# A written order of TensorE, VectorE and ScalarE in both attentions of a two-layer transformer kernel

## Chip, cores and metric

The kernel runs on one core of one Trainium2 chip. The metric is the device time in microseconds (us) of one execution. PE is TensorE, DVE VectorE, ACT ScalarE, POOL GpSimd, SP SyncE.

## What is computed

Eight sequences of 512 tokens with 256 features pass through two layers. Each layer is attention and then routed experts, each behind a layer norm and added to its input:

```python
x = x + _L0_attn_ref(_layernorm(x), Wq, Wk, Wv, Wo)      # 16 heads of 16, 4 kv heads, rope, causal
x = x + _L0_ffn_ref(_layernorm(x), router_w, ...)        # 32 experts, 8 for a token
x = x + _L1_attn_ref(_layernorm(x), w_qkv, b_qkv, ...)   # 16 heads of 16, causal
x = x + _L1_ffn_ref(_layernorm(x), gate_w, ...)          # 16 experts, 2 for a token, and a shared one
```

The softmax of the attention is computed as the exponential of the scores, a causal mask by multiplication, a product with v that has a column of ones beside it, and a division by that column's result.

## The kernel before, in words

**Stages.** A preamble of some 31 us, attention 0 with the router of layer 0, the experts of layer 0, attention 1 with the router and the shared expert of layer 1, the experts of layer 1 with the output. The change touches the two attentions. The experts run with their TensorE instructions in written order (L1173); everything else is put in order by a scheduler at compile time, which takes the program's order as a starting point and fills each engine's queue as it thinks fit. [...]

**Attention.** Both layers use the class `Attention` (L615 to L731). A sequence is done in four groups c of four heads (NCK = 4, NG = 4). The keys lie in four blocks j of 128; `BANKS = [[0], [1, 3], [2]]` puts them in three steps n[...]: j = 0 has 512 queries, 1 and 3 have 384 and 128, 2 has 256. A step is `scores` (L628): for each block four matmuls, one for each head, on 32 rows of the array each, so that four run side by side (L638), and one exponential over all four heads (L643) from PSUM tile `st`, of which there is one; then `mask` (L646): a multiplication of the diagonal blocks by the causal mask on DVE (L649). The tiles p of steps 0 and 1 share a tag with two buffers, that of step 2 has one.

`values` (L653) of a group: sixteen matmuls into `o` (L661; four for each block, on 32 columns each, so that four run side by side), a copy of `o` to SBUF on DVE (L667), four transposes to token order (L674), the reciprocal of the sums (L677), and the multiplication (L678 and on). It yields after each block, after the copy and at the end, and `steps` (L684) takes one such piece after the scores and one before the mask of each step of the next group. `output` (L707) of a sequence: two small operations on `fine` (L712, L713), transposes (L719) and copies (L720) to `oT`, the product with the output weights `y` (L727) and its addition to x (L731).

**Fills.** `pipeline` (L734) goes through the sequences. While the groups of sequence b run, it calls piece by piece `before(b + 1)` (the next sequence's load, layer norm, q, k and v) and `finish(b - 1)` (`output` and then `after`, the layer norm for the experts and the router of the sequence before). How many pieces have been made at which step is a matter of counts: `n_before` and `n_after` yields spread over the steps.
- `before` of layer 0 (L828): transposes of the input and copies `x_in` on ACT, layer norm, xT, `qkv` (L843), the rotation on DVE (L850 to L865, for each of four tiles of 128 tokens), transposes and copies of q and k (L873 to L883). Of layer 1 (L926): addition of the gathered experts' result (L932), layer norm, v (L941, L945), q (L954), k (L959 to L963).
- `layernorm` (L281): statistics of four tiles (bn_stats, bn_aggr, L286 to L288), `inverse_root` (L266; twelve small DVE operations, shift and three Newton steps), four tiles `xn` (L292). `turned` (L302): transposes to xT and copies on ACT.
- `route` (L314): logits `lg` (L321), the maximum (L327), an exponential on ACT (L336), choosing the best, the ranks `rk` by matmul (L368, L370), keys and row numbers (L382), and indirect DMAs on POOL that scatter the normalized rows `xn_f` to the experts' buffers (L385): 32 a sequence in layer 0, 8 in layer 1. The tag `xn_rows` has two buffers in layer 0 and one in layer 1.
- `shared` (L393), in layer 1: the shared expert, after `route`, with Silu on ACT (L406).
- `ahead1` in attention 1: for sequence b + 3, a fetch of its x, a part of a weight load, and `gathers` (L1197), that is row numbers on DVE and 32 indirect DMAs on POOL (L1200).

After the last sequence, its own `finish` runs with nothing beside it; the experts' loads of weights `dw` are issued after the last product with v.

Of the kernel before, what the change touches and what calls it, by code (L numbers as in the profile page):

```python
# [16 lines left out]
P = 128  # L17
# [55 lines left out]
STEPS = 2 * len(BANKS)  # L73
# [17 lines left out]
def two_blocks_kernel(  # L91
# [78 lines left out]
    def biases1(tmp, bank):  # L170
# [8 lines left out]
        yield  # L179
# [18 lines left out]
        yield  # L198
# [67 lines left out]
    def inverse_root(var, lnp, name):  # L266

        v = lnp.tile([P, NT], F32, tag="v", name=f"v_{name}")
        nc.vector.tensor_scalar(v, var, LN_EPS, None, ALU.add)
        bits = lnp.tile([P, NT], I32, tag="bits", name=f"bits_{name}")  # L270
        nc.vector.tensor_scalar(bits, v.bitcast(I32), 1, None, ALU.arith_shift_right)
        r = lnp.tile([P, NT], F32, tag="rstd", name=f"rstd_{name}")
        nc.vector.tensor_scalar(r.bitcast(I32), bits, -1.0, float(0x5F3759DF), ALU.mult, ALU.add)
        w = lnp.tile([P, NT], F32, tag="w", name=f"w_{name}")
        for _ in range(3):
            nc.vector.scalar_tensor_tensor(w, r, -0.5, r, ALU.mult, ALU.mult)
            nc.vector.tensor_tensor(w, w, v, ALU.mult)
            nc.vector.scalar_tensor_tensor(r, w, 1.5, r, ALU.add, ALU.mult)
        return r

    def layernorm(x, lnp, name, tag="xn", bufs=1, spare=0, behind=None):  # L281

# [6 lines left out]
        rstd = inverse_root(mv[:, :, 1], lnp, name)  # L289
        xn = lnp.tile([P, NT, D + spare], F32, tag=tag, name=f"xn_{name}", bufs=bufs)  # L290
        for t in range(NT):
            nc.vector.tensor_scalar(  # L292
                xn[:, t, :D], x[:, t, :], mv[:, t, 0:1], rstd[:, t : t + 1], ALU.subtract, ALU.mult
            )
        return xn

    def free():

        for _ in range(4):
            yield  # L300

    def turned(xn, lnp, bank, name):  # L302

        xT = lnp.tile([P, ND, T], F32, tag="xT", name=f"xT_{name}")
        for c in range(ND):
# [4 lines left out]
            yield  # L310
        return xT

    def ffn_parts(smp, bank):
        def route(n, b, xn, xT, name, again):  # L314
# [10 lines left out]
            yield  # L325
# [11 lines left out]
            yield  # L337
# [10 lines left out]
            yield  # L348
# [15 lines left out]
            yield  # L364
# [26 lines left out]
            yield  # L391

        def shared(w, xT, x, name):  # L393

            hs = smp.tile([P, NS, T], F32, tag="hs", name=f"hs_{name}", bufs=1)
            for n in range(NS):
# [11 lines left out]
                yield  # L408
            for half_ in range(NT // 2):
# [11 lines left out]
                yield  # L421
# [3 lines left out]
    def general_parts(awp, lnp, atp, ptp, smp, bank, vbias1=None):  # L425
# [130 lines left out]
        def attention0(b, w):  # L556
            x, name = xs[b], f"a0_{b}"
            xn = yield from turned(layernorm(x, lnp, name), lnp, bank, name)
# [34 lines left out]
        def attention1(b, w):  # L593
            x, name = xs[b], f"a1_{b}"
            xn = yield from turned(layernorm(x, lnp, name), lnp, bank, name)
# [19 lines left out]
    class Attention:  # L615
# [6 lines left out]
        def __init__(self, n, late, ptp, ps, bank, wo, masked=None):  # L622
            self.n, self.fine, self.late, self.ptp, self.ps, self.bank, self.wo = n, fines[n], late, ptp, ps, bank, wo
            self.heads, self.otok, self.rec = {}, {}, {}
            self.last = iter(())
            self.masked = masked

        def scores(self, b, c, n, probs):  # L628
# [13 lines left out]
            pt = self.ptp.tile([P, NG, width], F32, tag="p2" if n == 2 else "p01", name=f"p_{name}", bufs=1 + (n < 2))  # L642
# [10 lines left out]
        def values(self, b, c, probs):  # L653
# [4 lines left out]
            for step, j in enumerate((0, 1, 3, 2)):  # L658
# [6 lines left out]
                yield  # L665
            osb = late.tile([P, T], F32, tag="osb", name=f"osb_{name}", bufs=1)
            nc.vector.tensor_copy(osb, o)  # L667
            yield
# [4 lines left out]
            for t in range(NT):  # L673
                nc.tensor.transpose(ot[:, t * P : (t + 1) * P], osb[:, t * P : (t + 1) * P], ident)  # L674
# [7 lines left out]
            yield  # L682

        def steps(self, b):  # L684

            for c in range(NCK):  # L690
                probs = {}
                for n in range(len(BANKS)):
                    self.scores(b, c, n, probs)
                    next(self.last, None)
                    yield
                    if n == len(BANKS) - 1:
                        self.last = self.values(b, c, probs)
                    next(self.last, None)
                    yield
                    self.mask(n, probs)  # L700

        def flush(self):
            for _ in range(STEPS - 1):
                next(self.last, None)
                yield

        def output(self, b, x):  # L707
# [8 lines left out]
            for k in range(ND):  # L716
# [4 lines left out]
                yield  # L721
            for h in range(NT // 2):
# [9 lines left out]
                yield  # L732

    def pipeline(att, before, after, n_before, n_after, till, ahead=None, lead=0):  # L734
# [8 lines left out]

        n_steps = NCK * STEPS
        n_after += 4
# [939 lines left out]
```

## Time and profile before

| | |
|---|---|
| median of 3 runs | 1708.37 us (1708.31 to 1708.81) |
| the profiled execution | 1701.29 us, of which 1699.6 us span |
| PE busy | 1543.7 us, 91% of the span |
| DVE busy | 992.0 us, 58% |
| ACT busy | 650.7 us, 38% |
| POOL busy | 792.1 us, 47% |
| first scores of the eight sequences of attention 0 (us after the span's start) | 30.7, 73.5, 120.0, 164.8, 212.4, 257.8, 307.7, 351.5 |
| last product with v of attention 0 | 392.3 |
| first scores of the eight sequences of attention 1 | 884.5, 933.1, 996.1, 1059.1, 1122.2, 1191.1, 1261.9, 1324.9 |
| first transposes of layer 1's experts | 1425.5 |

The difference of two neighbours in these lists is the length of a sequence's window. An engine that is busy for nearly the whole window bounds it. A line of the timeline gives start, length, engine, source line, operation, output and inputs, shape and number of instructions, and in brackets how long the engine was idle before and what ended that.

### The profile page before, as it was taken

Reading aid. Unit: us, or ns where it says so; the run is one execution under the profiler, and the core shown is the slowest. Engines: PE = TensorE matmul, PEld = TensorE weight load, DVE = VectorE, ACT = ScalarE, POOL = GpSimd, SP = SyncE. Lnnn points to the kernel's source line nnn. Section 1 sums busy time; section 2 is a strip of 40 time slices with the busy share of each in tenths; the row PEclk is TensorE's granted clock in tenths of the full one; section 3 lists DMA queues with packets and bytes.
Section 4 is the critical chain, followed back from the end, with each engine's and each line's share of the span. In section 5 each row is a group of like instructions: output and inputs, shape, how many; then the busy total and the mean of one; then the engine's idle time right before and its main releaser. Section 6 shows DMA issues by size and latency. Waiting matters only on the chain. (4 is left out here: it accounts for less than half of the span.)

```text
span 1699.6 us, 30922 instructions
## 1 busy us (share of the span) xinstructions
PE 1543.7 (91%) x10180; PEld 1029.0 (61%) x10180; DVE 992.0 (58%) x3131; ACT 650.7 (38%) x865; POOL 792.1 (47%) x660
## 2 busy tenths in 40 slices
PE   5899999995999999999989999999899988999982
PEld 2455454543898999998853454544444545777761
DVE  5678887875555555555455764764656544444452
ACT  2555554552233333333334554454355331222221
POOL 0017677577710004888888448888511011000473
PEclk9999999997999999999999999999899998999996
DMA  2035557236988778999995245664312024343563
GB/s 73 13 87 156 163 167 270 102 139 207 307 256 269 202 201 226 266 264 273 268 194 71 39 107 80 127 136 72 86 52 79 26 84 159 109 159 116 156 225 120
DMA packets 255128, 259.43 MB, mean 153 GB/s; under 512 B 80212, under 2 KB 235988, under 8 KB 254964
## 3 DMA queue, kind: packets, MB, share of 16 engines
q1 hardware_dynamic: 199172, 167.88, 32.5%
q0 software_dynamic: 55296, 88.65, 23.0%
q8 instruction: 87, 1.43, 0.4%
q10 hardware_dynamic: 496, 0.85, 0.1%
q14 instruction: 77, 0.63, 0.1%
HBM read 132.70 MB, written 124.57 MB: 151 GB/s over the span
## 5 line engine op out<-in xcount | busy, mean ns | idle before, releaser
L1200 POOL DMA_INDIRECT x_a<-yg,yrows x256 | 402.9, 1574 | 277.2 <-DMA xg_m<-xg 181.9
L385 POOL DMA_INDIRECT xg<-xn_f,rows_f x320 | 321.2, 1004 | 414.7 <-DVE rows_f L382 197.3
L643 ACT ACTIVATE p_a<-st_a 128x2048 f32<-128x2048 f32 (+1 forms) x192 | 306.1, 1594 | 276.4 <-PE st_a L638 243.2
L1131 PE MATMUL gu_m<-gw,xgTs_m 128*128 x1552 | 335.6, 360 | 4.9 <-DVE xgTs_m L1108 3.0
L1131 PEld LDWEIGHTS gu_m<-gw,xgTs_m 128*128 128x128 f32 x1552 | 258.1, 192 | 33.9 <-DVE xgTs_m L1108 3.2
L1162 PE MATMUL y_m<-dw,hTs_m 96*128 (+1 forms) x952 | 237.7, 379 | 0.0
L638 PE MATMUL st_a<-qT_a,kT_a 32*128 32x512 f32 (+3 forms) x2048 | 202.1, 478 | 11.1 <-ACT p_a L643 10.8
L649 DVE TENSOR_TENSOR p_a<-p_a,causal 128x512 f32<-128x512 f32 x256 | 170.8, 686 | 57.3 <-ACT p_a L643 56.1
L661 PE MATMUL o_a<-p_a,v 128*32 128x512 f32 (+3 forms) x2048 | 197.4, 455 | 6.9 <-DVE p_a L649 6.7
L1108 DVE COPY xgTs_m<-xgT_m 128x512 f32<-128x512 f32 x194 | 133.9, 690 | 109.7 <-PE xgT_m L1106 109.4
L1167 ACT COPY ys_m<-y_m 128x512 f32<-128x512 f32 x194 | 113.7, 586 | 189.1 <-PE y_m L1162 174.7
L1123 DVE SCALAR_TENSOR_TENSOR h_m<-h_m,xg_m,gu_m 128x96 f32<-128x96 f32 (+1 forms) x388 | 114.8, 326 | 115.2 <-ACT h_m L1136 69.3
L1162 PEld LDWEIGHTS y_m<-dw,hTs_m 96*128 96x128 f32 (+1 forms) x952 | 165.3, 190 | 15.1
L1262 POOL DMA_INDIRECT g<-yg,yrows x64 | 65.2, 1018 | 202.2 <-DVE h_m L1123 170.9
L638 PEld LDWEIGHTS st_a<-qT_a,kT_a 32*128 32x128 f32 x2048 | 90.1, 189 | 107.2 <-issue 52.4
L1152 DVE COPY hTs_m<-hT_m 96x256 f32<-96x256 f32 (+1 forms) x194 | 92.7, 478 | 99.5 <-PE hT_m L1151 98.5
L1106 PE MATMUL xgT_m<-ident,xg_m 128*128 128x128 f32 x776 | 119.3, 275 | 16.0 <-DMA xg_m<-xg 13.2
L1139 ACT ACTIVATE h_m<-gu_m 128x192 f32<-128x192 f32 x150 | 49.7, 331 | 212.2 <-PE gu_m L1131 200.6
L1106 PEld LDWEIGHTS xgT_m<-ident,xg_m 128*128 128x128 f32 x776 | 95.6, 141 | 39.2 <-issue 16.6
L661 PEld LDWEIGHTS o_a<-p_a,v 128*32 128x32 f32 x2048 | 49.3, 110 | 107.8 <-issue 66.1
L1151 PE MATMUL hT_m<-ident,h_m 128*96 128x128 f32 (+1 forms) x476 | 84.9, 274 | 0.6 <-DVE h_m L1123 0.4
L667 DVE COPY osb_a<-o_a 128x512 f32<-128x512 f32 x64 | 44.0, 688 | 53.0 <-PE o_a L661 53.0
(198 smaller groups left out, 1689.6 us busy)
## 6 DMA issues: line engine op xcount, KB each, us to landing
yg<-ys_m SPq DMA_DIRECT2D x194, 256.0 KB
xg_m<-xg SPq DMA_DIRECT2D x300, 144.0 KB
xg_m<-xg SPq DMA_DIRECT2D x88, 136.0 KB
xg<-zeros SPq DMA_DIRECT2D x66, 144.0 KB
xg<-xn_f,rows_f POOLq DMA_INDIRECT x320
xg<-zeros SPq DMA_DIRECT2D x34, 136.0 KB
xf<-in_x_dram SPq DMA_DIRECT2D x8, 512.0 KB
x_after<-x_in SPq DMA_DIRECT2D x8, 512.0 KB
```

Of the source, the lines that this page charges most:

```text
L385: inst = nc.gpsimd.indirect_dma_start(out=lay.xg, out_offset=bass.IndirectOffsetOnAxis(ap=rows[:, t, i : i + 1], axis=0), in_=xn[:, t, :], ...
L638: nc.tensor.matmul(st[:, g, at : at + T - j * P], kT[r, j * P : (j + 1) * P], qT[r, j * P :], start=True, stop=True,)
L643: nc.scalar.activation(pt, st[:, :, :width], AF.Exp, scale=SCALE)
L649: self.masked = nc.vector.tensor_tensor(d, d, causal.unsqueeze(1).to_broadcast([P, NG, P]), ALU.mult).ins
L661: nc.tensor.matmul(o[32 * g : 32 * g + 32, j * P :], v1[:, j, v_at + g * (DH + 1) :][:, :32], probs[n][:, g, at : at + T - j * P], start=( ...
L1106: nc.tensor.transpose(tr[:, j, c, :], xg[:, j, c * P : (c + 1) * P], ident)
L1108: nc.vector.tensor_copy(xT, tr)
L1123: nc.vector.scalar_tensor_tensor(h[:, j, :], h[:, j, :], xg[:, j, D:][:, bass.ds(offs[part, i + j][2], 1)], gus[j][:, inner:], ALU.mult, A ...
L1131: nc.tensor.matmul(gus[j], xT[:, j, c, :], gu[:, bass.ds(at + c * 2 * inner, 2 * inner)], start=(c == 0), stop=(c == ND - 1),)
L1162: nc.tensor.matmul(y[:, j, :], hT[:n_in, q, j, :], dn[:n_in, bass.ds(at + q * D, D)], start=(q == 0), stop=(q == n_ch - 1),)
L1167: nc.scalar.copy(ys, y)
L1200: nc.gpsimd.indirect_dma_start(out=xs[b][:, t, :], out_offset=None, in_=yg, in_offset=rows, compute_op=ALU.add)
```

## The change

Both pipelines now stand in `tc.manual_schedule(engines={PE, DVE, Activation})`: these three engines' queues are in the order in which the program writes the instructions. POOL and SP are left to the scheduler. The program's own order changes with it:
- `values` becomes `products` (all sixteen matmuls in one go, and the copy of `o`, which moves from DVE to ACT) and `normalize` (transposes, reciprocal, multiplication). Of the group before, `products` stands after the scores of step 0 and `normalize` after those of step 1.
- A gap is the place between the scores of a step and its mask. Fills are made only in gaps 1 and 2 of a group. Each yield now carries a cost in us (negative: VectorE work on which the next piece waits; zero: nothing more in this gap). The class `Fill` counts cost against what is due at each gap, in the shares 0, 0.55 and 0.45, and at least `LEAST` is made in a gap.
- `layernorm` is a generator in six pieces: two of statistics, two of the root, two of normalizing.
- In layer 1 pieces of `route` and `shared` alternate, q and k have tiles of their own for each half (three buffers), and p of steps 0 and 1 have three buffers. `ahead` starts at gap 2 of a sequence and is called twice a gap.

The rest of the diff puts costs on yields. Its core:

```diff
@@ -70,7 +70,8 @@
 BANKS = [[0], [1, 3], [2]]
 QOFF = {0: (0, 0), 1: (1, 0), 3: (1, 3 * P), 2: (2, 0)}
-STEPS = 2 * len(BANKS)
+NGAP = NCK * len(BANKS)
+LEAST = (0.0, 1.6, 1.2)
 SUM_LO, SUM_HI = 1e-20, 1e30
@@ -286,18 +278,31 @@
             with tc.issue_after(behind) if behind else ExitStack():
                 nc.vector.bn_stats(out=stats[:, t, :], in_=x[:, t, :])
             nc.vector.bn_aggr(out=mv[:, t, :], in_=stats[:, t, :])
-        rstd = inverse_root(mv[:, :, 1], lnp, name)
+            if t % 2:
+                yield -1.1
+        v = lnp.tile([P, NT], F32, tag="v", name=f"v_{name}")
+        nc.vector.tensor_scalar(v, mv[:, :, 1], LN_EPS, None, ALU.add)
+        bits = lnp.tile([P, NT], I32, tag="bits", name=f"bits_{name}")
+        nc.vector.tensor_scalar(bits, v.bitcast(I32), 1, None, ALU.arith_shift_right)
+        r = lnp.tile([P, NT], F32, tag="rstd", name=f"rstd_{name}")
+        nc.vector.tensor_scalar(r.bitcast(I32), bits, -1.0, float(0x5F3759DF), ALU.mult, ALU.add)
+        w = lnp.tile([P, NT], F32, tag="w", name=f"w_{name}")
+        for n in range(3):
+            nc.vector.scalar_tensor_tensor(w, r, -0.5, r, ALU.mult, ALU.mult)
+            nc.vector.tensor_tensor(w, w, v, ALU.mult)
+            nc.vector.scalar_tensor_tensor(r, w, 1.5, r, ALU.add, ALU.mult)
+            if n != 1:
+                yield -1.1
         xn = lnp.tile([P, NT, D + spare], F32, tag=tag, name=f"xn_{name}", bufs=bufs)
         for t in range(NT):
             nc.vector.tensor_scalar(
-                xn[:, t, :D], x[:, t, :], mv[:, t, 0:1], rstd[:, t : t + 1], ALU.subtract, ALU.mult
+                xn[:, t, :D], x[:, t, :], mv[:, t, 0:1], r[:, t : t + 1], ALU.subtract, ALU.mult
             )
+            if t % 2:
+                yield -0.8
+        yield 0.0
         return xn
-    def free():
-        for _ in range(4):
-            yield
     def turned(xn, lnp, bank, name):
@@ -639,7 +647,7 @@
                         st[:, g, at : at + T - j * P], kT[r, j * P : (j + 1) * P], qT[r, j * P :],
                         start=True, stop=True,
                     )
-            pt = self.ptp.tile([P, NG, width], F32, tag="p2" if n == 2 else "p01", name=f"p_{name}", bufs=1 + (n < 2))
+            pt = self.ptp.tile([P, NG, width], F32, tag="p2" if n == 2 else "p01", name=f"p_{name}", bufs=3 if n < 2 else 1)
             nc.scalar.activation(pt, st[:, :, :width], AF.Exp, scale=SCALE)
             probs[n] = pt
@@ -662,16 +670,18 @@
                         o[32 * g : 32 * g + 32, j * P :], v1[:, j, v_at + g * (DH + 1) :][:, :32],
                         probs[n][:, g, at : at + T - j * P], start=(step == 0), stop=(step == NT - 1),
                     )
-                yield
-            osb = late.tile([P, T], F32, tag="osb", name=f"osb_{name}", bufs=1)
-            nc.vector.tensor_copy(osb, o)
-            yield
+            self.osb = late.tile([P, T], F32, tag="osb", name=f"osb_{name}", bufs=1)
+            nc.scalar.copy(self.osb, o)
+        def normalize(self, b, c, probs):
+            late, name = self.late, f"a{self.n}_{b}_{c}"
             if c == 0:
                 self.otok[b] = late.tile([P, NT, NCK, NG, DH], F32, tag="otok", name=f"otok_{name}", bufs=1)
                 self.rec[b] = late.tile([P, NCK, NT, NG], F32, tag="rec", name=f"rec_{name}", bufs=2)
             ot = self.bank(f"ot_{name}")
             for t in range(NT):
-                nc.tensor.transpose(ot[:, t * P : (t + 1) * P], osb[:, t * P : (t + 1) * P], ident)
+                nc.tensor.transpose(ot[:, t * P : (t + 1) * P], self.osb[:, t * P : (t + 1) * P], ident)
             ot = ot.rearrange("p (t g d) -> p t g d", t=NT, g=NG)
             rec = self.rec[b][:, c, :, :]
             nc.vector.reciprocal(rec, ot[:, :, :, ONE])
@@ -679,9 +689,9 @@
                 self.otok[b][:, :, c, :, :], ot[:, :, :, :DH],
                 rec.unsqueeze(3).to_broadcast([P, NT, NG, DH]), ALU.mult,
             )
-            yield
         def steps(self, b):
@@ -691,18 +701,15 @@
                 probs = {}
                 for n in range(len(BANKS)):
                     self.scores(b, c, n, probs)
-                    next(self.last, None)
-                    yield
-                    if n == len(BANKS) - 1:
-                        self.last = self.values(b, c, probs)
-                    next(self.last, None)
+                    if self.last:
+                        (self.products, self.normalize, lambda *_: None)[n](*self.last)
                     yield
                     self.mask(n, probs)
+                self.last = (b, c, probs)
         def flush(self):
-            for _ in range(STEPS - 1):
-                next(self.last, None)
-                yield
+            self.products(*self.last)
+            self.normalize(*self.last)
         def output(self, b, x):
@@ -729,9 +737,46 @@
                             start=(k == 0), stop=(k == ND - 1),
                         )
                 nc.vector.tensor_tensor(x[:, 2 * h : 2 * h + 2, :], x[:, 2 * h : 2 * h + 2, :], y, ALU.add)
-                yield
-    def pipeline(att, before, after, n_before, n_after, till, ahead=None, lead=0):
+                yield 1.75
+    class Fill:
+        def __init__(self, part, total, share, first, last):
+            self.part, self.total, self.first, self.last = part, total, first, last
+            whole = sum(share[k % len(BANKS)] for k in range(first, last + 1))
+            self.share = [total * s / whole for s in share]
+            self.gap = -1
+            self.at = self.due = 0.0
+            self.waits = False
+            self.held = -1
+        def pass_gap(self, n):
+            self.gap += 1
+            if self.gap >= self.first:
+                self.due += self.share[n]
+        def behind(self):
+            return (self.due - self.at) / self.total
+        def able(self):
+            if not self.part or self.gap < self.first or self.gap == self.held:
+                return False
+            return self.behind() > 0.0 or not self.waits
+        def make(self):
+            cost = next(self.part, None)
+            if cost is None:
+                self.part = ()
+                return 0.0
+            self.waits = cost < 0.0
+            if cost == 0.0:
+                self.held = self.gap
+            self.at += abs(cost)
+            return max(cost, 0.0)
+    def pipeline(att, before, after, t_before, t_after, share, ahead=None):
@@ -741,27 +786,39 @@
             yield from att.output(b, xs[b])
             yield from after(b)
-        n_steps = NCK * STEPS
-        n_after += 4
-        drain(before(0))
-        for b in range(NB):
-            pre = before(b + 1) if b + 1 < NB else iter(())
-            post = finish(b - 1) if b else iter(())
-            early = ahead(b + 3) if ahead and b + 3 < NB else iter(())
-            made_pre = made_post = 0
-            for n, _ in enumerate(att.steps(b)):
-                while made_post < n_after * (n + 1 - STEPS) // (till - STEPS):
-                    next(post, None)
-                    made_post += 1
-                while made_pre < n_before * (n + 1 - lead) // (n_steps - 2 - lead):
-                    next(pre, None)
-                    made_pre += 1
-                next(early, None)
-            drain(pre)
-            drain(post)
-            drain(early)
-        drain(att.flush())
-        drain(finish(NB - 1))
+        with tc.manual_schedule(engines={ENG.PE, ENG.DVE, ENG.Activation}):
+            drain(before(0))
+            fills = []
+            for b in range(NB):
+                if b:
+                    last = NGAP + 1 if b + 1 < NB else NGAP - 1
+                    fills.append(Fill(finish(b - 1), t_after(b - 1), share, 2, last))
+                if b + 1 < NB:
+                    fills.append(Fill(before(b + 1), t_before, share, 0, NGAP - 2))
+                early = ahead(b + 3) if ahead and b + 3 < NB else iter(())
+                for k, _ in enumerate(att.steps(b)):
+                    filled = 0.0
+                    for fill in fills:
+                        fill.pass_gap(k % len(BANKS))
+                    while k % len(BANKS):
+                        able = [f for f in fills if f.able()]
+                        if not able:
+                            break
+                        fill = max(able, key=lambda f: f.behind())
+                        if fill.behind() <= 0.0 and filled >= LEAST[k % len(BANKS)]:
+                            break
+                        filled += fill.make()
+                    for fill in [f for f in fills if f.gap > f.last]:
+                        drain(fill.part)
+                        fills.remove(fill)
+                    if k > 1:
+                        next(early, None)
+                        next(early, None)
+                drain(early)
+            for fill in fills:
+                drain(fill.part)
+            att.flush()
+            drain(finish(NB - 1))
     def load_out(pool, src, cols, load):
@@ -945,26 +1001,27 @@
-            qT = atp.tile([P, 2, T], F32, tag="qT", name=f"qT_{name}")
-            kT = atp.tile([P, 2, 2, T], F32, tag="kT", name=f"kT_{name}")
+            qT, kT = [], []
+                qT.append(atp.tile([P, T], F32, tag="qT", name=f"qT_{name}_{m}", bufs=3))
+                kT.append(atp.tile([P, 2, T], F32, tag="kT", name=f"kT_{name}_{m}", bufs=3))
-            att.heads[b] = lambda c: (qT[:, c // 2, :], kT[:, c // 2, c % 2, :], v1, c * NG * (DH + 1))
+            att.heads[b] = lambda c: (qT[c // 2], kT[c // 2][:, c % 2, :], v1, c * NG * (DH + 1))
@@ -1399,7 +1455,9 @@
             if b == SPLIT[0] - 1:
                 yield from tables(lays[0][0], smp, bank, False)
-        pipeline(att, before, after0, 15, 12, 22)
+        pipeline(
+            att, before, after0, 17.5, lambda b: 19.8 + (b == 1) + 5.0 * (b == SPLIT[0] - 1), (0.0, 0.55, 0.45)
+        )
     with ExitStack() as s1:
@@ -1425,17 +1483,21 @@
             def after1(b):
                 name = f"f1_{b}"
-                xn = layernorm(xs[b], lnp, name, "xn_rows", 1, E1)
-                yield from free()
+                xn = yield from layernorm(xs[b], lnp, name, "xn_rows", 1, E1)
                 xT = yield from turned(xn, lnp, bank, name)
-                yield from route(1, b, xn, xT, name, False)
-                yield from shared(w1["s"], xT, xs[b], name)
+                routed, beside = route(1, b, xn, xT, name, False), shared(w1["s"], xT, xs[b], name)
+                for made in (routed, beside, routed, routed, beside, routed, routed, routed, routed):
+                    yield next(made)
+                drain(routed)
+                yield from beside
                 if b < NB - 1:
                     keep_x(b, x_after[1])
                 if b == SPLIT[1] - 1:
                     yield from tables(lays[1][0], smp, bank, False)
-            pipeline(att, before, after1, 15, 17, NCK * STEPS, ahead1, 4)
+            pipeline(
+                att, before, after1, 17.5, lambda b: 32.4 + 4.0 * (b == SPLIT[1] - 1), (0.0, 0.55, 0.45), ahead1
+            )
             out_of = not_fine(bank)
```

## Prediction

> **What bounds the kernel now.** I read the page's busy table first (TensorE 91%, VectorE 58%, ScalarE 38%), then the busy time of each engine in windows that I cut from the first scores of one sequence to the first scores of the next, then the timeline of one window, and last GpSimd's timeline in the second attention. The change touches only the two attentions, about 31 to 392 us and 885 to 1425 us; the experts between and after them have the same instructions in the same order.
>
> ```profile
> core 0: us, PE busy (x) PEld busy (x) DVE busy (x) ACT busy (x) POOL busy (x), PEclk, DMA share, GB/s
> 120.00:164.80 44.80, 42.25 (x367) 22.47 (x366) 37.31 (x139) 25.39 (x25) 32.09 (x33) 1.00 0.55 168
> 212.40:257.80 45.40, 42.79 (x363) 22.19 (x362) 37.88 (x143) 25.23 (x24) 33.10 (x32) 1.00 0.55 173
> 996.10:1059.10 63.00, 61.10 (x417) 31.52 (x416) 39.26 (x127) 31.11 (x28) 46.59 (x29) 1.00 0.57 99
> 1122.20:1191.10 68.90, 62.94 (x421) 32.84 (x420) 39.41 (x127) 31.11 (x28) 57.01 (x40) 0.95 0.60 112
> ```
>
> Each row: start and end, length, then the busy time of PE, PE's loads, DVE, ACT and POOL. A sequence of attention 0 takes about 45 us, of which PE is busy 42 to 43: it bounds, and DVE follows at 83%. The six middle sequences last 278.0 us (73.5 to 351.5), so 46.3 each, PE busy 44.2, idle 2.1. In attention 1 one takes 63.0 with PE at 97%, except the fifth and sixth (68.9, 70.8), where POOL (57 us busy) is the limit.
>
> ```profile
> 207.21 1.88 ACT L643 ACTIVATE p_a<-st_a 128x2048 f32<-128x2048 f32 x1 [0.88 <-PE st_a L638]
> 208.67 1.05 PE L661 MATMUL o_a<-p_a,v 128*32 128x512 f32 x2
> 209.12 1.36 DVE L649 TENSOR_TENSOR p_a<-p_a,causal 128x512 f32<-128x512 f32 x2
> 210.29 1.92 PE L661 MATMUL o_a<-p_a,v 128*32 128x512 f32 x22
> 217.22 1.07 PE L661 MATMUL o_a<-p_a,v 128*32 128x512 f32 x8
> ```
>
> Two things are to be seen (start, length, engine, line). The exponential ends at 209.09 and its mask starts at 209.12: before, the mask goes ahead of all other VectorE work. And the products with v: two matmuls alone take 1.05, eight together 1.07.
>
> [...] the two rows just named agree (groups of four overlap, a broken group pays nearly twice). [...] The trace's records agree in that starts follow the program; my whole argument rests on it, since the change writes that order. [...] the trace has loads of 1283 ns.
>
> **The change, part by part.** The orders of before and after have the same matmuls, the same POOL order and nearly the same SP order.
>
> *Products in one go.* In a sequence of attention 0 about 1.2 groups of four (scores or products) were cut by other matmuls, and each cut costs one more us (1.05 for two, as shown). After has none: PE's work falls from 44.2 to 43.0, that is −1.2 a sequence; attention 1 had hardly any.
>
> *The copy of o from VectorE to ScalarE.* −4 × 0.69 on DVE, +4 × 0.58 on ACT (55% busy): nothing on PE. If ACT were late, it would delay the next exponential by 0.58.
>
> *Masks behind the fills.* This is the step that decides. In after's VectorE order mask n stands behind everything filled into its gap: with p = 1 it waits for normalization, statistics, additions; with p = 2 for the rest. The products of a group now stand in one block after the next group's first scores (1.07), so the third bank must be masked 1.07 + 1.0 + 1.0 = 3.07 us after these start. What is queued behind a waiting product on PE is everything. I followed one sequence (the seventh) through the four head groups. Durations from before's rows: scores 1.07, 1.08, 0.64; products 1.0, 1.0, 0.57; exponentials 1.88, 1.88, 1.02; mask 0.67; statistics of one sequence 1.8; twelve small operations of the root 2.4; normalizing a tile 0.37; addition 0.62; rotation of a tile 1.6; qkv of a tile 1.53; y 1.85 a half; logits 2.1.
> - Group 0: the input's copies wait behind exponential 1 (8.2 us after the group's start, to 9.35), statistics to 10.7, masks of bank 1 to 12.0, keys 1.4, fine 0.4, root 2.4, mask 2 at 16.9. PE would take the last product at 13.6. Stall 3.3.
> - Group 1: y's second half ends at 22.8, addition and normalizing to 24.2 (xT's transposes lose 0.8), statistics and masks to 26.5, half a root, mask 2 at 29.3 against 28.4. Stall 0.8 + 0.9 = 1.7.
> - Group 2: after the first qkv, three rotations 4.8, half a root 1.2 and four tiles 1.5 put mask 1 at 41.9 (PE there at 40.4), a rotation and mask 2 at 44.2 (42.9). Stall 1.5 + 1.3 = 2.8.
> - Group 3: logits end at 51.8, choosing takes 3.8, mask 2 at 56.4 against 54.9. Stall 1.5.
>
> The sum is 9.3, and 43.0 + 9.3 = 52.3 for a sequence, against 46.3. From the other side: VectorE has 34.9 us of work, some 6.4 in which it must wait for the transposed o (four times product 0.57, copy, scores 1.08, transposes 0.52, less the mask beside them), and 4.8 to 6 in which a fill waits for its own qkv, y or logits: 46 to 48. The truth lies between, since a late group's fill finds its inputs ready and the sequences aren't all cut alike; I take 50: +3.7 each, six times, +22 us (ends: +2 × 6 = +12 if only VectorE's sum counts; +6 × 6 = +36; and −12 if the stalls don't come, see below). The first sequence has no normalization behind it and gains the clock-slow idle it has now (42.8 us for 35.9 busy): −3. The last pays what remains (its router's rank matmuls stand ahead of its last products and wait for the choosing), and the experts' 48 weight loads wait for its last product (at 392.3 the first is issued), so that they start later by as much: +4. Attention 0: +23.
>
> *Attention 1, TensorE.* One sequence needs 60.7 of PE. The same reading gives stalls in the first two groups only: 2.6 (statistics, masks, root, gather keys before mask 2) and 4.3 (two additions, normalizing, statistics, twelve root operations, two masks, four tiles before mask 2). 67 instead of 63.0.
>
> *Attention 1, GpSimd.* Its order is unchanged, but its gathers of later sequences need row numbers that VectorE makes (ykey), and those moved.
>
> ```profile
> 895.42 1.94 POOL L1200 DMA_INDIRECT x_a<-yg,yrows  x1 [0.30 <-DVE mv_a L288]
> 1003.97 1.58 POOL L1200 DMA_INDIRECT x_a<-yg,yrows  x1 [17.65 <-DVE p_a L649]
> 1065.12 1.03 POOL L385 DMA_INDIRECT xg<-xn_f,rows_f  x1 [0.30 <-DVE fine L712]
> 1208.53 1.03 POOL L385 DMA_INDIRECT xg<-xn_f,rows_f  x1 [0.30 <-issue]
> 1149.95 1.38 DVE L292 TENSOR_SCALAR xn_f<-x_a,mv_f,rstd_f 128x256 f32<-128x256 f32 x4 [4.11 <-DMA xg<-xn_f,rows_f]
> ```
>
> In before, the fifth sequence's gather starts at 895.4, 38 us ahead of the second sequence (933.1); the scatter of the fourth ends at 1218.5, 285 us after 933.1, and the last row shows the cost: one buffer of normalized rows, so the next normalization waits for the scatter. In after, the row numbers stand in group 0 of the second sequence: the gather starts about 14 us into it, then four times 72 us (gathers 60.6, scatter 10.6, measured) gives 302 us. The seventh sequence then starts some 10 us later than now, and this covers PE's own loss up to there (five times 4 less the 13.7 that POOL costs already = 6). With +3 in the seventh, −4 in the first (48.6 us for 41.8 busy), −3 in the tail (the shared expert fills the wait for the chosen rows): +6.
>
> *Table loads.* 16 more in the program, 20 us on ACT, which is 40 to 50% busy in attention 1: I take nothing; without that cover 1.28 each, +20. *Buffers* (a third p tile, halves of qT and kT): they only allow the order. Clock: [...] in the rows 0.95 and less; not counted.
>
> Sum: 23 + 6 = +29 on 1701.3 (span 1699.6 and 1.7 around it) = 1730.3. The median is 7.1 over the profiled run: 1737.4.
>
> **Rivals.** *Faster: the masks come in time.* Then the cuts are gone (−12), half of the 2.1 idle goes (−6), and the first and last pieces gain (−7, of which POOL's delay takes back about 7): −18, or 1690. For it: PE is at 95% and VectorE has 8 us free in a sequence. Against it: the written order itself. It decides in group 0: between exponential 1's end (8.2) and the last product (13.6) there are 5.4 us, and VectorE has 8.7 us of work before mask 2. If it needs under 5.4, this rival wins. *Only part of it counts:* the stalls eat the cuts and no more in attention 0, and POOL's +6 remains: +3 to +12, 1715. *All of it:* every stall in full (+36 − 3 + 4 = +37), attention 1 +10: 1755. *The change does not do what it says:* excluded, the orders show it.
>
> **Numbers.** Chances: forecast 0.54 (1722 to 1748), all of it 0.14, part 0.13 (mostly slower, 0.05 within 0.2% of now), faster 0.19. About 0.2% is what a measurement can tell from no change. Faster 0.19, same 0.05, slower 0.76. The range reaches to 1700 and 1757; below lie most of the faster cases (0.14), above 0.06. The likeliest's own range is 1722 to 1748.
>
> **What would show it.** Right: VectorE's masks of bank 2 start 2 to 6 us after their exponential; the last product of a group waits for the mask (some 1 to 3 us, summed over attention 0 about 55 us); windows of 49 to 52 us; POOL's fifth gather after the second sequence's start. Wrong: masks within a us, windows of 44 to 45; or idle of PE put down to ACT, which I took as hidden.

## The result, and the profile after

The changed kernel takes 1802.1 us (median of 4, 1799.85 to 1805.18), the kernel before beside it 1708.34 (1703.23 to 1708.81): ratio 1.056, interval 1.053 to 1.059. The prediction had the direction, but not the size: +94 us where it said +29, and 45 us above its range. The profiled execution took 1805.18 us, its span is 1803.3.

The busy table of the changed kernel, first:

```profile
PE 1554.1 (86%) x10180; PEld 1062.9 (59%) x10180; DVE 980.5 (54%) x3067; ACT 706.1 (39%) x945; POOL 794.8 (44%) x660
```

PE has 10 us more of busy time for the same matmuls, though the cut groups are gone, and 5 points less of the span. Then four windows, from the first scores of one sequence to those of the next (columns as in the prediction): the fourth and seventh of attention 0, the third and sixth of attention 1.

```profile
178.90:235.00 56.10, 45.36 (x379) 26.62 (x378) 38.23 (x142) 27.91 (x29) 36.40 (x35) 0.91 0.45 143
353.10:409.10 56.00, 44.34 (x376) 25.39 (x375) 37.16 (x133) 27.30 (x28) 32.21 (x32) 0.91 0.28 99
1070.70:1142.50 71.80, 63.82 (x419) 34.24 (x418) 39.35 (x130) 35.71 (x34) 56.70 (x38) 0.93 0.58 106
1286.00:1355.10 69.10, 61.94 (x417) 33.98 (x416) 37.97 (x123) 35.72 (x34) 16.10 (x15) 0.95 0.16 44
```

The seventh sequence of attention 0 in the kernel before:

```profile
307.70:351.50 43.80, 43.59 (x389) 23.06 (x388) 40.45 (x149) 25.22 (x24) 31.68 (x31) 1.00 0.36 126
```

There TensorE was busy for nearly the whole window, at a granted clock (the column after POOL) of 1.00. In the two windows of attention 0 no engine is busy for more than 81% now, and the clock is 0.91. By stage, in us, from the starts of the scores, in the two profiled executions (their spans differ by 103.7, the medians by 94):

| | before | after | change | predicted |
|---|---|---|---|---|
| attention 0, first sequence | 42.8 | 41.7 | −1 | −3 |
| six middle ones | 278.0 | 335.3 | +57 | +22 |
| last, to its last product | 40.8 | 51.2 | +10 | +4 |
| attention 1, first | 48.6 | 43.9 | −5 | −4 |
| six middle ones | 391.8 | 426.9 | +35 | +13 |
| last, to the experts | 100.6 | 105.0 | +4 | −3 |

The rest, experts included, differs by some 2 in all. Eight of the runs below were taken on chips on which the kernel before took 2012 or 2025 us, and three of their kernels were run again where it took 1703 to 1705 us.

The timeline of TensorE in the seventh sequence, first two head groups (start, length; in brackets the idle time before and what ended it):

```profile
353.05 1.14 PE L646 MATMUL st_a<-qT_a,kT_a 32*128 32x512 f32 x8
354.12 1.93 PE L669 MATMUL o_a<-p_a,v 128*32 128x512 f32 x24
358.24 0.64 PE L669 MATMUL o_a<-p_a,v 128*32 128x256 f32 x8 [2.19 <-DVE p_a L657]
358.81 1.15 PE L646 MATMUL st_a<-qT_a,kT_a 32*128 32x384 f32 x16
...
363.86 1.14 PE L646 MATMUL st_a<-qT_a,kT_a 32*128 32x512 f32 x8
364.93 1.93 PE L669 MATMUL o_a<-p_a,v 128*32 128x512 f32 x24
370.53 0.84 PE L669 MATMUL o_a<-p_a,v 128*32 128x256 f32 x8 [3.67 <-DVE p_a L657]
371.30 2.09 PE L646 MATMUL st_a<-qT_a,kT_a 32*128 32x384 f32 x16
```

In most groups the last eight product records wait for the third mask, as foretold (2.19 and 3.67 us; I had 1.5 and 3.3). What I had not priced stands in the last line: the same sixteen score matmuls take 1.15 us after the shorter wait, at a granted clock of 1.00 (358.81 to 359.96), and 2.09 after the longer, at 0.50 (371.30 to 373.39). And ScalarE and VectorE between these two products:

```profile
362.78 1.03 ACT L651 ACTIVATE p_a<-st_a 128x1024 f32<-128x1024 f32 x1
365.07 1.88 ACT L651 ACTIVATE p_a<-st_a 128x2048 f32<-128x2048 f32 x1 [0.30 <-PE st_a L646]
369.71 0.16 DVE L293 SCALAR_TENSOR_TENSOR rstd_a<-w_a,rstd_a 128x4 f32<-128x4 f32 x1
369.79 1.29 DVE L657 TENSOR_TENSOR p_a<-p_a,causal 128x512 f32<-128x512 f32 x2
374.45 0.26 DVE L687 RECIPROCAL rec_a<-ot_a 128x16 f32<-128x16 f32 x1 [3.37 <-PE ot_a L684]
```

The first group's third exponential is done at 363.81, but its mask starts at 369.79, together with the next group's first, behind the last operation of the root. Then VectorE stands idle for 3.37 us until the transposed o comes. TensorE waits for the mask, VectorE for the product: each of the two is idle while the other works. The third mask starts 4.9 us after its exponential now, 0.6 us in the kernel before (medians of the 32 groups of attention 0), and the waits of the products for masks sum to 60.7 us in attention 0.

### The profile page after: what moved, and what is told of

The parts are those of the page before. It is cut to its first block, busy times and chain, and to the rows that moved or that the text cites. A ratio compares the mean times of both kernels' runs of the same rounds, so it can differ in the third digit from the quotient of the medians.

```text
span 1803.3 us, 30910 instructions
## 1 busy us (share of the span) xinstructions
PE 1554.1 (86%) x10180; PEld 1062.9 (59%) x10180; DVE 980.5 (54%) x3067; ACT 706.1 (39%) x945; POOL 794.8 (44%) x660
## 5 line engine op out<-in xcount | busy, mean ns | idle before, releaser
L392 POOL DMA_INDIRECT xg<-xn_f,rows_f x320 | 323.1, 1010 | 488.8 <-DVE fine L719 198.2
L669 PE MATMUL o_a<-p_a,v 128*32 128x512 f32 (+3 forms) x2048 | 177.5, 472 | 96.8 <-DVE p_a L657 96.8
L646 PE MATMUL st_a<-qT_a,kT_a 32*128 32x512 f32 (+3 forms) x2048 | 216.2, 518 | 24.7 <-ACT p_a L651 23.4
L657 DVE TENSOR_TENSOR p_a<-p_a,causal 128x512 f32<-128x512 f32 x256 | 166.3, 683 | 53.6 <-ACT p_a L651 51.9
L669 PEld LDWEIGHTS o_a<-p_a,v 128*32 128x32 f32 x2048 | 55.7, 115 | 234.9 <-DVE p_a L657 133.7
L646 PEld LDWEIGHTS st_a<-qT_a,kT_a 32*128 32x128 f32 x2048 | 96.8, 205 | 125.4 <-issue 58.9
L674 ACT COPY osb_a<-o_a 128x512 f32<-128x512 f32 x64 | 37.5, 586 | 159.5 <-PE o_a L669 159.5
L687 DVE RECIPROCAL rec_a<-ot_a 128x16 f32<-128x16 f32 x64 | 16.5, 257 | 133.5 <-PE ot_a L684 133.5
```

The source lines that it names most:

```text
L392: inst = nc.gpsimd.indirect_dma_start(out=lay.xg, out_offset=bass.IndirectOffsetOnAxis(ap=rows[:, t, i : i + 1], axis=0), in_=xn[:, t, :], ...
L646: nc.tensor.matmul(st[:, g, at : at + T - j * P], kT[r, j * P : (j + 1) * P], qT[r, j * P :], start=True, stop=True,)
L657: self.masked = nc.vector.tensor_tensor(d, d, causal.unsqueeze(1).to_broadcast([P, NG, P]), ALU.mult).ins
L669: nc.tensor.matmul(o[32 * g : 32 * g + 32, j * P :], v1[:, j, v_at + g * (DH + 1) :][:, :32], probs[n][:, g, at : at + T - j * P], start=( ...
```

## The experiments

The theory: the 94 us come from VectorE's written order, in which masks stand behind the fills, by waits of the products and by the slow clock after some of these (0.50, as just shown). Rivals: ScalarE's written order with the copy of o in it; TensorE's written order; the amount of VectorE's work whatever the place of the masks.

**Which written order it is.** Three runs take one or two engines out of the written order, one line each:

```diff
-        with tc.manual_schedule(engines={ENG.PE, ENG.DVE, ENG.Activation}):
+        with tc.manual_schedule(engines={ENG.PE, ENG.Activation}):   # e1; e2 {PE, DVE}; e3 {PE}
```

> The changed kernel, but VectorE's order in both attentions is left to the scheduler; TensorE's and ScalarE's stay as written (TensorE's queue is the same, instruction for instruction). Theory: the masks that stand behind the fills in VectorE's queue cost the 94 us, partly as waits of the products with v[...]. Then most of it comes back: 1690 to 1725 us, the wait of the products for the mask falls from 97 us to under 30. Rival A (ScalarE's written order, with the copy of o in it): 1790 to 1805. Rival B (TensorE's written order itself): 1770 to 1805.

> The changed kernel, but ScalarE's order is left to the scheduler; TensorE's and VectorE's stay as written. Theory (masks behind fills on VectorE): no change worth speaking of, 1780 to 1805 us. Rival A (ScalarE's written order): 1700 to 1740.

> The changed kernel with only TensorE's order written; VectorE and ScalarE are left to the scheduler. Theory (masks behind fills): as without VectorE's written order, 1690 to 1725 us. Rival B (TensorE's written order): 1770 to 1805 still.

Measured: 1672.9 (VectorE free), 1805.4 (ScalarE free), 1680.5 (only TensorE written), beside 1704.8 for the kernel before; one run each. TensorE's 10180 records stand in the same order in all of them. The whole loss, and more, is in VectorE's order; ScalarE's costs nothing (1673 with it, 1681 without) and TensorE's is no loss. The waits of the run with VectorE free, VectorE's for the transposed o and TensorE's for the masks (total us, times, longest):

```profile
DVE rec_a L687 <- PE ot_a L684: 60.0, 40, 3.0
...
PE o_a L669 <- DVE p_a L657: 11.6, 14, 1.7
```

In the changed kernel, and then in the kernel before:

```profile
DVE rec_a L687 <- PE ot_a L684: 133.5, 64, 3.6
...
PE o_a L669 <- DVE p_a L657: 96.8, 50, 3.7
...
DVE rec_a L677 <- PE ot_a L674: 20.2, 23, 3.2
...
PE o_a L661 <- DVE p_a L649: 6.7, 13, 2.7
```

**The place of the masks.**

```diff
                     self.scores(b, c, n, probs)
 ...
-                    yield
                     self.mask(n, probs)
+                    yield
```

> The changed kernel with each mask written ahead of the fill of its gap instead of behind it; all three orders are written. Theory (masks behind fills): the products no longer wait for masks, but now VectorE stands before each mask until the exponential is done and the fill comes later, so that the fills' own consumers wait instead: between, 1720 to 1770 us. Rival C (the position of the masks is not what matters, VectorE has simply too much in a row): 1790 and above.

Measured: 1720.7. Of the 129 us between the changed kernel and the one with VectorE free, moving the masks alone takes 81; products wait 23.5 us for masks instead of 96.8. The other 48 are not taken apart. Against the run with VectorE free, with the same matmuls in the same order, TensorE is busy for 18 us more (1515.5 for 1497.3) and idle for 30 more. VectorE now stands 105.3 us before masks until their exponentials are done (51.9 in the changed kernel), but it does so for 84.9 us when it is free, too.

**One gap or all of the row.** The fills go from the third gap to the second (`LEAST` 0, 1.6, 0; shares 0, 0.9, 0.1).

> The changed kernel with the fills moved from the third gap of a group to the second (shares 0, 0.9, 0.1 instead of 0, 0.55, 0.45; no minimum in the third gap). Theory: what counts is all VectorE work between the second exponential and the third mask, and that stays the same: 1775 to 1830 us. Rival E (it is the fill right ahead of the third mask): below 1750.

> Fills moved from the third gap to the second once more, for the same reason. Theory (all VectorE work between the second exponential and the third mask counts, wherever it stands): 1775 to 1830 us. Rival E (the fill right ahead of the third mask): below 1750. The parts of the first run without scatters (49.7 against 51.9, 67.4 against 73.3) point to a little faster, 1770 to 1790.

> Fills moved from the third gap to the second, on a chip whose scatters are not slowed. Theory (all VectorE work between the second exponential and the third mask counts, wherever it stands): 1775 to 1830 us. Rival E (the fill right ahead of the third mask): below 1750.

Measured: 2091.9 (beside 2012), 2118.5 (beside 2025) and 1790.3 (beside 1703). In the last of these the six middle sequences of attention 0 take 336.1 us against 335.3: moving the fill away from the third mask, to the gap before, brings nothing there, so Rival E is out. (The matmuls of the fills move with them, so TensorE's queue is not the same.) The six middle sequences of attention 1 took 17 us less; why was not followed up.

**The clock.** Twelve transposes of the identity, never read, stand ahead of products that wait, at five places in each sequence of attention 0 and two in each of attention 1 (the list `WARM`):

```diff
+                if (j, self.n, c) in WARM:
+                    warm = self.bank(f"warm_{name}_{j}")
+                    for i in range(3 * NT):
+                        nc.tensor.transpose(warm[:, i % NT * P : (i % NT + 1) * P], ident, ident)
```

> The changed kernel, with twelve additional transposes of the identity (about 1.5 us, never read) ahead of the products that wait for a mask: 56 such places, 87 us of added TensorE work, of which 60 to 75 would lie in the waits. Theory with the clock [...]: the same matmuls elsewhere get 30 to 50 us shorter, 1765 to 1795 us in spite of the added work. Rival D (only the waits themselves cost): 1812 to 1835.

> The kernel with added transposes once more, since in its first run the scatters of attention 0 took about twice their time and the kernel before 2012 us. As before: with the clock 1765 to 1795 us; Rival D (only the waits themselves cost) 1812 to 1835. From the parts of the first run that had no scatter (second sequence of attention 0: 51.7 against 51.9; second of attention 1: 69.2 against 73.3) I lean to the first.

> The kernel with added transposes on a chip whose scatters are not slowed (the first two runs had before at 2012 and 2025 us). With the clock 1765 to 1800 us; Rival D (only the waits themselves cost) 1812 to 1835.

Measured: 2106.6 (beside 2012), 2119.1 (beside 2025) and 1804.2 (beside 1705), so neither. (These expectations speak of slowed scatters. The traces do not show that: one scatter takes 1010 ns on average in the changed kernel, 971 in the run with VectorE free and two buffers beside 2012 us and 978 in the run of the kernel before with products in one go beside 2025 us. What stands out in these two are long waits of ScalarE before an exponential, of up to 24.9 and 26.9 us between 120 and 400 us, and their cause is open.) From the first scores of attention 0 to its last product, in the last of the three runs and then in the changed kernel:

```profile
31.10:464.20 433.10, 385.43 (x3368) 229.32 (x3368) 277.81 (x982) 211.31 (x212) 195.70 (x192) 0.95 0.35 112
```

```profile
32.00:460.40 428.40, 342.22 (x2888) 191.24 (x2888) 277.35 (x979) 212.77 (x213) 193.41 (x189) 0.90 0.35 112
```

At forty places 61.5 us of transposes were added (480 records), yet PE's busy time rose by 43.2: its own 2888 records became 18 us shorter at the higher clock (0.95 for 0.90). But the six middle sequences took 332.9 us against 335.3. Most of the added work fell into waits (products wait 42.1 us for masks in this run, 96.8 in the changed kernel), and the 18 us that were saved do not show either: TensorE is not the bound any more. What goes round, by the timeline above, is the chain mask, last product, copy, transposes, VectorE's fill, mask. A slow product or transpose lengthens that chain, but how much of the 94 us the clock costs in this way stays open: the added transposes can themselves hold up a product whose mask is there.

**Products one step later**, after the next group's second scores:

> The changed kernel, all three orders written, but a group's products with v stand one step later (after the second scores of the next group, with its exponential behind their first block; the copy and the normalization follow one step later too). Masks stay behind the fills. Theory: a product then has about a step more before it needs the third mask, so the waits for masks (97 us on TensorE) fall below 40 and with them the slow clock: 1720 to 1760 us. Rival C (VectorE has too much in a row, wherever the product stands): 1785 and above.

It ran only beside 2012 us for the kernel before: 2165. In its second sequence, which has no scatters beside it, 56.2 us against 51.9: slower. The second exponential stands behind the first block of products here, and the waits show it (ScalarE's exponential for o, 200 us), so the run does not test what it should.

**What of the change is good.**

```diff
-        with tc.manual_schedule(engines={ENG.PE, ENG.DVE, ENG.Activation}):
+        with ExitStack():
```

> The changed program with no order written at all: the scheduler has all engines, as in the kernel before, but products in one go, the copy on ScalarE, pieces and buffers are those of the changed kernel. Theory: it is TensorE's written order that gives the gain over the kernel before when VectorE is free (1672), since the scheduler cuts groups and puts products early: 1685 to 1710. Rival: the products in one go and the copy's move give it: 1668 to 1680.

Measured: 1692.6 beside 1702.9. With TensorE's and ScalarE's order written and VectorE free, timed:

> VectorE left to the scheduler, timed against the kernel before in rounds. Where before takes about 1705 us: 1668 to 1678 us, ratio 0.98. Theory: nothing of the change but VectorE's written order is slower than before.

1672.2 us, ratio 0.981 (0.978 to 0.983). So of some 32 us about 10 come from products, copy, pieces and buffers, and 20 from the written orders of TensorE (12 by the run with only its order written) and ScalarE. Left to itself, the scheduler cuts groups of four products with other matmuls at 57 places, and TensorE is busy for 1547.5 us; with the written orders and VectorE free none is cut, and TensorE is busy for 1497.3. And products in one go are shorter: from start to next start, 32 records take 2.29 us in the changed kernel (at 423.00 us), in three pieces before 1.00 + 1.00 + 0.57 = 2.57 (at 326.19, 328.85 and 332.42).

> The kernel before with one part of the change alone: a group's sixteen products with v stand in one go in the program (their pieces' places in the sequence are kept, empty); everything is left to the scheduler. Theory (cut groups of four cost about a us each, some twenty of them in attention 0): 1690 to 1700 us, 8 to 15 less than before on the same chip. Rival (the scheduler cuts them again, or the products then wait for the last mask): 1703 to 1715.

This ran only beside 2025 us for the kernel before (2088, ratio 1.033). Here the products stand ahead of the third mask, so the third bank is multiplied without its mask, and the mask waits for the products. Nothing follows from it.

**GpSimd's chain.** With VectorE free, the fourth to sixth sequence of attention 1 took 69.8, 71.7 and 71.7 us, and VectorE waited for scatters before it could normalize (three waits of 9.2 to 11.1 us there):

```profile
DVE xn_f L298 <- DMA xg<-xn_f,rows_f: 35.2, 8, 11.1
```

One number is changed in `after1`: `"xn_rows", 1` to `"xn_rows", 2`.

> The changed kernel with VectorE left to the scheduler, and two buffers instead of one for the normalized rows in layer 1. In the run with VectorE free the fourth to sixth sequence of attention 1 took 70 to 72 us against 60 for the others, each with a wait of the normalization for the scatter of the sequence before. Theory (GpSimd's chain of gathers and scatters binds there through that one buffer): 1640 to 1655 us. Rival (GpSimd's gathers themselves are late for the sequence that reads them): 1665 to 1675.

> VectorE left to the scheduler and two buffers of normalized rows in layer 1, once more. Theory (GpSimd's chain binds through that one buffer in the fourth to sixth sequence of attention 1): these take 60 to 66 us instead of 70 to 72, in all 1640 to 1655 us. Rival (the gathers themselves are late for the sequence that reads them): 1665 to 1675.

> VectorE left to the scheduler and two buffers of normalized rows in layer 1. With one buffer: 1672 us, and 69.8, 71.7 and 71.7 us for the fourth to sixth sequence of attention 1. Theory (GpSimd's chain binds there through the one buffer): these take 60 to 66 us, in all 1640 to 1660. Rival (the gathers themselves are late for the sequence that reads them): 1665 to 1675.

Measured: 1990.4 (beside 2012, ratio 0.988, 0.986 to 0.991), 2005.1 (beside 2025, ratio 0.991, 0.989 to 0.994), and 1642.1 us (beside 1703, ratio 0.965, 0.962 to 0.968): the fastest version here. The fourth to sixth sequence in it:

```profile
1030.70:1090.30 59.60, 58.03 (x417) 32.46 (x416) 36.78 (x123) 35.55 (x34) 49.54 (x34) 1.00 0.61 117
1090.30:1149.90 59.60, 58.03 (x417) 32.49 (x416) 36.81 (x123) 35.55 (x34) 49.54 (x34) 1.00 0.61 117
1149.90:1209.50 59.60, 58.03 (x417) 32.48 (x416) 36.72 (x123) 35.55 (x34) 49.55 (x33) 1.00 0.51 92
```

59.6 each, PE at 97% and at a clock of 1.00, with gathers still beside them: the one buffer was the bound.

## Why the prediction was wrong in size

- **Masks behind the fills: right, and under-sized.** For the seventh sequence I had followed stalls of 3.3, 1.7, 2.8 and 1.5 us; the waits for masks and normalized tiles there are 3.67, 1.81, 3.45 and, for the group before, 2.19. Of the signs named, the third mask's distance (4.9 us for 2 to 6) and the sum of the waits (60.7 us for about 55) came true, the windows did not (51.9 to 61.1 us for 49 to 52). I had 43.0 of work and 9.3 idle; measured are 44.3 and 11.7, 56.0 for 52.3. That the work fits so well is luck: with VectorE free the same matmuls are busy for 40.0 in this sequence, at a clock of 1.00. I had 3 too much of work, and nothing for the slow clock (scores 2.09 for 1.15, transposes 1.09 for 0.66) and the overlap lost at waits, which made 4.4.
- **The step that failed: "I take 50".** I set the followed sum back, halfway towards VectorE's total (46 to 48), because late fills would find their inputs ready. They did not: the chain closes on itself, a late mask makes the next group's transposed o late. VectorE's waits in that window sum to 17.1 us, of which 10.6 for the transposed o (I had 6.4) and 6.5 for the fills' inputs (4.8 to 6); with 37.2 busy (34.9) that is 54.3 of 56.0. The six middle sequences took 55.9 on average. Of the 35 us that I missed there, 14 come from taking 50 instead of 52.3, and 21 from the followed sum itself, which was short.
- **"Clock: not counted" failed too.** With the same queue, PE is busy for 1554.1 us in the changed kernel and for 1497.3 with VectorE free; these 57 us are not work. Some 48 of them are rate, by an estimate from the records of the granted clock: 183 us of busy time fall in stretches at a clock of 0.50, 88 with VectorE free, and I count half of the difference as lost, since the scores take 2.09 us there for 1.15. The rest I put down to overlap lost where a wait splits the products (1.93 + 0.64 for 2.36). How much of them is in the time stays open in attention 0, as the added transposes show.
- **The last sequence of attention 0:** +10 for +4. TensorE is busy for 40.8 us there, at a clock of 0.83, and for 35.0 with VectorE free and the same matmuls: 5.7 of its length stand in busy time that is no work. Most of it I take for rate, which I had not counted: 15.2 us of the busy time lie in stretches at a clock of 0.50.
- **Attention 1, TensorE:** 67 foretold, 69.1 where no gather is beside it and 71.8 where VectorE makes the gather's row numbers as well. Of 71.8 in the third sequence it is busy for 63.8 and idle for 8.0, where I had 60.7 and 6.9; with VectorE free it is busy for 58.1, at a clock of 1.00. Most of the miss stands in the busy time, and I put it down to the rate again, which I had taken as nothing: the clock is 0.93 in that window, and 9.2 us of the busy time lie in stretches at 0.50.
- **Attention 1, GpSimd: wrong as the bound there.** I let its chain cover TensorE's loss. The chain itself came as foretold: the fifth gather started 14.1 us into the second sequence (14), and the scatter behind the eighth ended 305 us into it (302). Of the later gathers only the sixth stood still, for 3.9 us; the others followed the scatter within 0.3. But no normalization waited for a scatter, the last one came 10 us after it: the sequences had grown by as much through VectorE. The two losses added nothing to each other, the larger one ruled, and it was VectorE's. The chain is real: it bounds once VectorE is free, as the run with two buffers shows.
- **Cut groups: right in sign, too small.** Estimated −1.2 a sequence. In the six middle sequences of the kernel before 13 groups were cut, two each, and blocks that follow each other overlap too (2.29 for 2.57). The third, fifth and seventh sequence had 42.3, 42.8 and 43.6 of PE work before and have 39.5, 40.5 and 40.0 with VectorE free, some −3.
- **Table loads: no cost seen.** 23 + 8 + 15 in attention 1 instead of 30, of 1.28 us each, and the run with VectorE free has the same 46 and is faster than before. With only TensorE's order written the 16 are gone, and the time is not shorter (1680.5). What the copy on ScalarE costs by itself was not measured.
- **Slips that changed little.** The rival "faster" takes −12 for the cuts, but six times 1.2 is 7. In GpSimd's sum 302 less 285 is 17, and it is not said how this becomes 10. And that the mask goes ahead of all other VectorE work before was read from one mask; in attention 0 the third mask starts up to 8.6 us after its exponential.

## What to carry to other kernels

An order written for an engine is only as good as its worst neighbour in the queue: put the operation that another engine waits for ahead of the fillers (81 us here), or leave that engine to a scheduler that does, and write only the order of the engine that bounds. Where two engines wait for each other in turn, add the larger side of each turn: in the one sequence followed here that came nearer (52.3 for 56.0) than a value between their totals (50). When a wait has been removed, look for the next one-buffer chain: here it was worth another 30 us.

## What was not expected of the hardware

A product wait of 3.67 us was followed by matmuls at a granted clock of 0.50 (scores 2.09 for 1.15, transposes 1.09 for 0.66); so were two waits of 1.67 and 1.78 within 5 us (0.50 from 400.61 to 402.70), while one of 3.58 was not (1.00 from 270.68 to 271.83; all in the changed kernel):

```profile
396.74 1.07 PE L669 MATMUL o_a<-p_a,v 128*32 128x384 f32 x16 [1.67 <-DVE p_a L657]
399.60 1.08 PE L669 MATMUL o_a<-p_a,v 128*32 128x256 f32 x8 [1.78 <-DVE p_a L657]
400.61 2.09 PE L646 MATMUL st_a<-qT_a,kT_a 32*128 32x384 f32 x16
...
270.11 0.64 PE L669 MATMUL o_a<-p_a,v 128*32 128x256 f32 x8 [3.58 <-DVE p_a L657]
270.68 1.15 PE L646 MATMUL st_a<-qT_a,kT_a 32*128 32x384 f32 x16
```

Waits of one length, 2.19 us, were followed by scores of 1.15 us at a clock of 1.00 (behind the product at 358.24) and of 1.68 at 0.64 (behind the one at 130.86). So in these cases the length of the wait does not tell by itself how fast the matmuls behind it run; what does was not shown. The sixteen products of a group in one go take 11% less than in three pieces (2.29 us against 2.57, from start to next start).
